# A mask moved from TensorE to VectorE, two heads' small operations joined, and a float8 product one unit later

## The chip, the cores and the metric

The kernel runs on one core of one Trainium2 chip. The metric is device time of one execution in microseconds (us). A core has five engines that work side by side, each through its own instructions in order: TensorE (PE, matrix products, with weight loads listed as PEld), VectorE (DVE), ScalarE (ACT), GpSimd (POOL) and SyncE (SP, which here only issues DMAs). They wait for each other through semaphores. Matrix products are written to PSUM, a small memory of eight banks; a bank holds 512 float32 per partition.

## The reference, cut to what matters

Input `x` is 4 batches of 1024 tokens with 512 features. The output is `x + attention(layernorm(x)) + float8_product(layernorm(x))`. Per batch, 16 heads of width 128:

```python
q  = rope(rmsnorm(xn @ Wq + bq));  lk = rope(rmsnorm(xn @ Wlk + blk));  lv = xn @ Wlv + blv
entries = softmax-weighted means of 4 tokens each            # 256 per batch
ck = rope(rmsnorm(entries @ Wk + bk));  cv = entries @ Wv + bv
sc = q @ ck.T * scale, where an entry that ends after the token gets -1e30
sparse = softmax over the 8 largest sc, times their cv
sl = q @ lk.T * scale over the token's own and the previous 128 tokens, masked to a band
local  = softmax(sl) @ lv
out = ((sparse + local) * 0.5) @ Wo + bo
```

The float8 branch rounds `xn * scale` and `input2 * scale1` to float8 values, and multiplies what was rounded.

## The kernel before, in words

A chunk is 128 tokens; there are 32 chunks `t`, 8 to a batch (`c` = 0 to 7). A unit is one pair of heads of one chunk: 8 units to a chunk (`u` = 0 to 7), 256 in all, numbered `n`. The tokens of a chunk sit in the 128 partitions. One main loop (L791) runs over steps `s`; the order of the instructions on every engine is exactly the order of the program. A step issues, for different units, a software pipeline:

- `scores(s, 0)` and `(s, 1)` (L563): TensorE writes, for each head, one 512-wide float32 PSUM tile `sc`: columns 0 to 127 scores with the previous chunk's keys (absent at `c` = 0), 128 to 255 with the own chunk's keys, and from 256 on the `m` = 32(c+1) compressed entries. A last small product, identity times mask (L583), adds -1e30 to the newest 32 entries that lie in the future. The tag `sc` has two buffers, one bank each.
- `keep_context(s-2)` (ACT), then `weigh(s, h)` for each head (L592): VectorE adds the band mask to the window's columns and finds the row's largest (L605), takes the eight largest entries (L608), negates the first (L610) and marks the eight taken ones in `taken` (`match_replace`, L611); ScalarE takes the exponentials of the window (L612) and of the entries (L620) from `sc` into `prob`.
- `queries(s+3)` (L440): TensorE's largest product, 8 instructions of 512 columns and a bias product.
- `settle(s, h)` (L623): VectorE zeroes the entries not taken and sums them (L627), guards and inverts the two sums (L636, L637), scales the entries (L638).
- `steps()`: one step of each running background generator: `chunk_prep` (layernorm, the entries of the chunk two ahead, 17 steps from `u` = 7) and `chunk_eight` (the float8 branch).
- `squares(s+3)` (ACT, L296) and `spread` (POOL: 1/sqrt by power, L290 and L291); `settle_window(s, h)` (ACT, L643, scales the window); `to_output(s-2)` (PE, L753); a second `steps()`.
- `turn(s)` (DVE, L661) transposes `prob` in 32x32 blocks and SP writes it to DRAM (L669); `values_of(s+1)` (PE, L537, into the shared two-buffer tag `pp`); `normalize(s+3)` (DVE L467, L310 to L312, with GpSimd's half of the rotation L309); `values(s-1)` (PE, L720, reads `probT` that came back from DRAM by `fetch`, L703); `turn_keys` and `fetch_keys` of `s+3`; `keep_values(s+1)` (ACT, L549).

The two background generators run in this way. `chunk_prep` of the chunk two ahead starts at `u` = 7 (layernorm statistics, L329, and 1/sqrt on GpSimd), normalizes at the next `u` = 0 (L337), turns at 1, multiplies at 2 (ScalarE copies the product `yp` to `y`, L361, then VectorE reads a column of it into `logits`, L363), ends at the next `u` = 7 with `cp`, copied by VectorE to `ckT` (L412, L414). `chunk_eight` of the own chunk starts at `u` = 5: three VectorE operations (L262 to L266) and GpSimd additions (L267, L269, L271, L273) at `u` = 5 and 6, the product `fp` (L425) in the first `steps()` of `u` = 7 and `f` (L430, L431) in the second. At `u` = 1 of the next chunk `to_output` adds the finished output to the residual (L762).

Of the kernel before, what the change touches and what calls it, by code (L numbers as in the profile page):

```python
# [12 lines left out]
F32 = mybir.dt.float32  # L13
BF16 = mybir.dt.bfloat16
U32 = mybir.dt.uint32
AF = mybir.ActivationFunctionType
ALU = mybir.AluOpType
AX = mybir.AxisListType

P = 128  # L20
# [10 lines left out]
TAKEN = 3e38  # L31
TAKEN_FROM = 1e38
# [6 lines left out]
def kernel(  # L39
# [26 lines left out]
    nc = tc.nc  # L66
# [5 lines left out]
    NE = P // RATIO  # L72
    NT = B * NCH
# [3 lines left out]
    const = ctx.enter_context(tc.tile_pool(name="const", bufs=1))  # L77
    work = ctx.enter_context(tc.tile_pool(name="work", bufs=2))
# [98 lines left out]
    picks = const.tile([P, NE], F32, name="picks")  # L177
    ident = const.tile([P, P], F32, name="ident")
    make_identity(nc, ident)
    ident_b = const.tile([P, P], BF16, name="ident_b")  # L180
    inv = const.tile([P, 1], F32, name="inv")
    bias_b = const.tile([P, 512], BF16, name="bias_b")
    nc.vector.memset(bias_b, 0.0)
# [250 lines left out]
    units = {}  # L434
# [115 lines left out]
        w["lv"] = lv  # L550


    heads = {}
    probs = [work.tile([P, 512], F32, name=f"prob_{h}", bufs=1) for h in range(2)]

    def columns(n):
# [6 lines left out]
    def scores(n, h):  # L563
        t, _ = place(n)
        c, m, loc, spa = columns(n)
        w = units[n]
        qT, lkT = w["qT"], w["lkT"]
        ckT, _ = entries[t // NCH]
        sc = psum.tile([P, 512], F32, tag="sc", name=f"sc_{n}_{h}")
        q = qT[:, :, h]  # L570
        if c:
            nc.tensor.matmul(
                blocks(sc[:, 0:P]),
                q,
                units[n - NU]["lkT"][:, :, ds(h * BLK, BLK)],
                start=True,
                stop=True,
            )
        nc.tensor.matmul(  # L579
            blocks(sc[:, P : 2 * P]), q, lkT[:, :, ds(h * BLK, BLK)], start=True, stop=True  # L580
        )
        nc.tensor.matmul(sc[:, spa], q, ckT[:, 0:m], start=True, stop=False)  # L582
        nc.tensor.matmul(  # L583
            sc[:, ds(2 * P + m - NE, NE)],
            ident_b,
            mask_b[:, 2 * P : 2 * P + NE],
            start=False,
            stop=True,
        )
        heads[n, h] = {"sc": sc}  # L590

    def weigh(n, h):  # L592
        c, m, loc, spa = columns(n)
        w = heads[n, h]
        sc = w.pop("sc")
        top = work.tile([P, 8], F32, tag="top", name=f"top_{n}_{h}")
        neg = work.tile([P, 2], F32, tag="neg", name=f"neg_{n}_{h}")
        tot = work.tile([P, 2], F32, tag="tot", name=f"tot_{n}_{h}", bufs=3)
        taken = work.tile([P, 2 * P], BF16, tag="taken", name=f"taken_{n}_{h}")
        prob = probs[h]  # L600
        if n % (NU * NCH) == 0:

            nc.gpsimd.memset(prob[:, 2 * P + NE : 4 * P], 0.0)

        nc.vector.tensor_tensor_reduce(  # L605
            sc[:, loc], sc[:, loc], mask_b[:, loc], -1.0, TAKEN, ALU.add, ALU.min, neg[:, 0:1]
        )
        nc.vector.max(top, sc[:, spa])  # L608

        nc.vector.tensor_scalar(neg[:, 1:2], top[:, 0:1], -1.0, 1e29, ALU.mult, ALU.min)  # L610
        nc.vector.match_replace(taken[:, 0:m], top, sc[:, spa], TAKEN)  # L611
        nc.scalar.activation(  # L612
            prob[:, loc],
            sc[:, loc],
            AF.Exp,
            bias=neg[:, 0:1],
            scale=-1.0,
            accum_out=tot[:, 0:1],
        )
        nc.scalar.activation(prob[:, spa], sc[:, spa], AF.Exp, bias=neg[:, 1:2])  # L620
        w.update(tot=tot, taken=taken, prob=prob)

    def settle(n, h):  # L623
        c, m, loc, spa = columns(n)
        w = heads[n, h]
        tot, taken, prob = w["tot"], w["taken"], w["prob"]
        nc.vector.scalar_tensor_tensor(  # L627
            prob[:, spa],
            taken[:, 0:m],
            TAKEN_FROM,  # L630
            prob[:, spa],
            ALU.is_ge,
            ALU.mult,
            accum_out=tot[:, 1:2],
        )
        nc.vector.tensor_scalar(tot, tot, 1e-9, None, ALU.max)  # L636
        nc.vector.reciprocal(tot, tot)  # L637
        nc.vector.tensor_scalar(prob[:, spa], prob[:, spa], tot[:, 1:2], None, ALU.mult)  # L638

    def settle_window(n, h):  # L640
        _, _, loc, _ = columns(n)
        prob, tot = heads[n, h]["prob"], heads[n, h]["tot"]
        nc.scalar.mul(prob[:, loc], prob[:, loc], tot[:, 0:1])  # L643

    def parts_of(n):

# [7 lines left out]
    def turn(n):  # L654
        parts = parts_of(n)
        g = len(parts)
        pb = work.tile([P, 1024], F32, tag="probB", name=f"probB_{n}", bufs=1)
        pb = of_heads(pb, n)
        for h in range(2):
            prob = heads.pop((n, h))["prob"]  # L660
            nc.vector.transpose(  # L661
                pb[:, :, ds(h * g, g), :],
                prob[:, parts[0] * P : (parts[-1] + 1) * P].rearrange(
                    "p (g b i) -> p b g i", b=NB, i=BLK
                ),
            )
        turned = dram.tile([P, 1024], F32, tag="pr", name=f"pr_{n}")
        turned = turned[:, 0 : NB * 2 * g * BLK]
        nc.sync.dma_start(turned, pb.rearrange("p b g i -> p (b g i)"))  # L669
        units[n]["pr"] = turned  # L670

    def turn_here(n):

        w, parts = units[n], parts_of(n)
        g = len(parts)
        w["tp"] = []
        for h in range(2):
            prob = heads.pop((n, h))["prob"]
            if h and g == 2:
                tp = tp[:, g * P :]  # L680
            else:
                tp = pp(f"tp_{n}_{h}")
            for i in range(g):
                nc.tensor.transpose(tp[:, ts(i, P)], prob[:, ts(parts[i], P)], ident)
            w["tp"].append(tp[:, 0 : g * P])
# [92 lines left out]
    def for_unit(n, *todo):  # L778
        if 0 <= n < NN:
            for f, *more in todo:  # L780
                f(n, *more)

    first, rounding = chunk_prep(0), round_w2()
    until(first, "A1")
    nc.vector.tensor_copy(ident_b, ident)
    until(first, "B2")
    small_constants()
    pick_tokens()
# [2 lines left out]
    for s in range(-3, NN + 2):  # L791
        t, u = place(s)

        if s == -2 or u == 7 and 0 <= t and t + 2 < NT:
            running = [*running[-2:], chunk_prep(t + 2)]
        if u == 3 and 0 <= t < NT:
            load_x(t, "sum")
        if u == 5 and 0 <= t < NT:
            running = [*running[-2:], chunk_eight(t)]
        if u == 4 and 0 <= t and t + 2 < NT:  # L800
            load_x(t + 2, "norm")

        for_unit(s, (scores, 0), (scores, 1))
        for_unit(s - 2, (keep_context,))
        for_unit(s, (weigh, 0), (weigh, 1))
        for_unit(s + 3, (queries,))
        if s + 2 < NU:
            for_unit(s + 2, (turn_keys_here,))
        for_unit(s, (settle, 0), (settle, 1))
        if s < 0:  # L810
            until(first, ("B3", "B4", "B6")[s + 3])
        steps()
        for_unit(s + 3, (squares, (0, 1, 2, 3)), (spread,))
        if s + 2 < NU:
            for_unit(s + 2, (keep_keys,))
        for_unit(s, (settle_window, 0), (settle_window, 1))
        for_unit(s - 2, (to_output,))
        steps()
        if by_dma(s):
            turn(s)  # L820
        if s == -1:
            until(first, "B7")
        for_unit(s + 1, (values_of,))
        if s == -1:
            until(first, "B8")
        if not by_dma(s):
            for_unit(s, (turn_here,))
        for_unit(s + 3, (normalize,))
        for_unit(s - 1, (values,))
        if by_dma(s):  # L830
            fetch(s)
        else:
            for_unit(s, (keep_turned,))
        if s + 3 >= NU:
            for_unit(s + 3, (turn_keys,), (fetch_keys,))
        for_unit(s + 1, (keep_values,))
        if s < NU:

            if s == -1:
                late_constants()  # L840
                for k in range(KK):
                    nc.scalar.dma_start(w2_raw[k], input2[ts(k, P), :])
            if 0 <= s < KK:
                for _ in range(4):
                    next(rounding, None)
            if 3 <= s + 6 < NU:
                load_wqk(s + 6, nc.scalar)
            if 3 <= s + 4 < NU:
                load_wlv(s + 4, nc.scalar)
            if 0 <= s + 1 < NU:  # L850
                load_wo(s + 1, nc.scalar)
        if u == 6 and 0 <= t and t + 2 < NT:
            load_angles(t + 2)
        units.pop(s - 1 - NU, None)
# [46 lines left out]
```

## Time and profile before

| | |
|---|---|
| time, median of 3 runs | 2831.97 us (2831.59 to 2832.27) |
| the profiled execution's own time | 2833.53 us |
| its span, first to last instruction | 2831.6 us |
| granted TensorE clock | 0.997 |
| busy: PE / DVE / ACT / POOL | 98% / 79% / 46% / 29% |
| DMA | 399.85 MB, 141 GB/s |

The span is the profiled execution from the first to the last instruction; the execution's own time is 1.9 us longer, and that time is 1.6 us above the median. A line of groups gives source line, engine, operation, tiles (out<-in), shape and count, then busy us and mean ns. A line of waits says who waited for whom: us in total, times, longest. A line of the timeline gives start, duration, engine and operation, and in brackets the idle time before it and what ended it. Busy shares are averages over the whole span.

### The profile page before, as it was taken

How to read it: one execution, taken by the hardware profiler on the slowest of the kernel's cores; microseconds unless marked ns; L12 is line 12 of the kernel's file. 1: busy time of each engine (PE TensorE's matmuls, PEld its weight loads, DVE VectorE, ACT ScalarE, POOL GpSimd, SP SyncE). 2: the span in 40 equal slices, each digit the busy share in tenths (PEclk: the TensorE clock that was granted, in tenths of full speed). 3: DMA queues.
4: the chain of work that ended last, by engine and by line, in shares of the span. 5: the costliest groups of instructions: out<-in, count | busy, mean ns of one | idle time of the engine just before them, and what ended most of it. 6: DMA issues, size and time to landing. Idle time of an engine off the chain costs nothing. (4 is left out here: it accounts for less than half of the span.)

```text
span 2831.6 us, 48506 instructions
## 1 busy us (share of the span) xinstructions
PE 2769.0 (98%) x12771; PEld 1873.8 (66%) x12969; DVE 2247.1 (79%) x9132; ACT 1299.1 (46%) x5075; POOL 821.3 (29%) x1161
## 2 busy tenths in 40 slices
PE   6999999999999999999999999999999999999998
PEld 4666666666666666666666666666666666667666
DVE  5777888888777778888877787888887777888886
ACT  3445444444444454444444444444444444444443
POOL 3432232322233322233223333223222233322221
PEclk9999999999999999999999999999999999999999
DMA  7345455555445445555544444555554544555553
GB/s 230 90 138 138 133 143 152 144 150 153 127 124 139 137 133 152 144 151 149 149 126 131 134 135 134 155 148 149 146 149 122 135 136 131 136 152 155 143 149 108
DMA packets 620850, 399.85 MB, mean 141 GB/s; under 512 B 306880, under 2 KB 573984, under 8 KB 620576
## 3 DMA queue, kind: packets, MB, share of 16 engines
q1 hardware_dynamic: 608352, 383.18, 48.8%
q10 hardware_dynamic: 12224, 13.56, 1.5%
q8 instruction: 105, 1.72, 0.3%
q14 instruction: 169, 1.38, 0.2%
HBM read 212.53 MB, written 184.03 MB: 140 GB/s over the span
## 5 line engine op out<-in xcount | busy, mean ns | idle before, releaser
L445 PE MATMUL qp<-wqk,xnT 128*128 128x512 f32 x2048 | 945.5, 604 | 4.9 <-DMA scales<-in_L_ffn_scale_dram 3.3
L445 PEld LDWEIGHTS qp<-wqk,xnT 128*128 128x128 f32 x2048 | 370.6, 191 | 385.2 <-issue 371.5
L612 ACT ACTIVATE prob<-sc,neg 128x256 f32<-128x256 f32 (+1 forms) x512 | 236.0, 461 | 779.6 <-DVE taken L611 759.3
L537 PEld LDWEIGHTS vp<-wlv,xnT 128*128 128x128 f32 x2048 | 386.5, 190 | 188.7 <-issue 94.0
L537 PE MATMUL vp<-wlv,xnT 128*128 128x256 f32 x2048 | 487.0, 381 | 17.2 <-DVE ckT L414 11.9
L753 PE MATMUL op<-wo,cT 128*128 128x512 f32 x1024 | 484.9, 596 | 7.1 <-ACT cT L735 1.5
L290 POOL TENSOR_SCALAR r<-ss 128x4 f32<-128x4 f32 x256 | 49.8, 194 | 1067.3 <-ACT junk L296 1059.3
L661 DVE STREAM_TRANSPOSE probB<-prob 128x512 f32<-128x512 f32 (+2 forms) x494 | 282.4, 609 | 92.5 <-ACT prob L643 89.1
L467 DVE SCALAR_TENSOR_TENSOR th<-qp,r,norm_w 128x128 f32<-128x128 f32 x1024 | 283.6, 339 | 71.0 <-POOL r L291 70.2
L309 POOL TENSOR_TENSOR rb<-th,cs 128x256 f32<-128x256 f32 x256 | 247.0, 965 | 278.0 <-DVE th L467 277.9
L296 ACT ACTIVATE junk<-qp 128x128 bf16<-128x128 f32 x1024 | 284.1, 277 | 88.0 <-remote 42.7
L549 ACT COPY lv<-vp 128x256 f32<-128x256 f32 x256 | 95.5, 373 | 477.6 <-PE cp L720 420.0
L753 PEld LDWEIGHTS op<-wo,cT 128*128 128x128 f32 x1024 | 188.9, 190 | 188.4 <-issue 113.9
L720 PE MATMUL cp<-probT,lv 128*128 128x128 f32 x1920 | 299.4, 276 | 4.4 <-DMA probT<-pr 4.4
L720 PEld LDWEIGHTS cp<-probT,lv 128*128 128x128 f32 x1920 | 276.1, 193 | 18.1 <-issue 5.2
L291 POOL TENSOR_TENSOR r<-r,nhalf 128x4 f32<-128x4 f32 x256 | 259.6, 1014 | 21.4
L720 PE MATMUL cp<-probT,cv 128*128 128x128 f32 x1536 | 256.7, 276 | 0.0
L582 PE MATMUL sc<-ckT,qT 128*128 128x96 f32 (+7 forms) x1024 | 226.5, 303 | 0.0
L643 ACT ACTIVATE prob<-prob,tot 128x256 f32<-128x256 f32 (+1 forms) x512 | 223.0, 484 | 3.6 <-DVE tot L637 3.6
L720 PEld LDWEIGHTS cp<-probT,cv 128*128 128x128 f32 x1536 | 214.3, 193 | 0.0
L605 DVE CUSTOM_DVE_ANT_0 sc<-sc,mask_b 128x256 f32<-128x256 f32 (+1 forms) x512 | 202.6, 396 | 7.2 <-PE sc L583 6.6
L579 PE MATMUL sc<-lkT,qT 128*128 128x128 f32 x1024 | 207.8, 285 | 0.0
(123 smaller groups left out, 3858.3 us busy)
## 6 DMA issues: line engine op xcount, KB each, us to landing
pr<-probB SPq DMA_DIRECT2D x127, 512.0 KB, 2.6
probT<-pr SPq DMA_DIRECT2D x508, 128.0 KB, 2.9
qk<-thb SPq DMA_DIRECT2D x992, 64.0 KB, 2.0
pr<-probB SPq DMA_DIRECT2D x96, 384.0 KB, 2.6
probT<-pr SPq DMA_DIRECT2D x384, 96.0 KB, 2.4
qT<-qk SPq DMA_DIRECT2D x248, 128.0 KB, 2.3
lkT<-qk SPq DMA_DIRECT2D x248, 128.0 KB, 2.5
x_norm<-_attn_hidden_states_dram SPq DMA_DIRECT2D x32, 256.0 KB, 3.2
```

The source lines that it names most:

```text
L291: nc.gpsimd.tensor_tensor(r, r, nhalf[: ss.shape[0], 0:n], ALU.pow)
L296: nc.scalar.activation(junk[: src.shape[0]], src, AF.Square, accum_out=acc)
L309: nc.gpsimd.tensor_tensor(bb, x12, wide(cs[:, HALF:ROPE]), ALU.mult)
L445: nc.tensor.matmul(qp, xnT[:, k, :], wqk_sb[u][:, k, :], start=(k == 0), stop=False)
L467: nc.vector.scalar_tensor_tensor(th[:, i, :], qp[:, ts(i, D)], r[:, i : i + 1], norm_w[:, i // 2, :], ALU.mult, ALU.mult,)
L537: nc.tensor.matmul(vp[:, 0:256], xnT[:, k, :], wlv_sb[u][:, k, :], start=(k == 0), stop=(k == KK - 1),)
L582: nc.tensor.matmul(sc[:, spa], q, ckT[:, 0:m], start=True, stop=False)
L612: nc.scalar.activation(prob[:, loc], sc[:, loc], AF.Exp, bias=neg[:, 0:1], scale=-1.0, accum_out=tot[:, 0:1],)
L643: nc.scalar.mul(prob[:, loc], prob[:, loc], tot[:, 0:1])
L661: nc.vector.transpose(pb[:, :, ds(h * g, g), :], prob[:, parts[0] * P : (parts[-1] + 1) * P].rearrange("p (g b i) -> p b g i", b=NB, i=BLK),)
L720: nc.tensor.matmul(blocks(cp[:, h, :]), v, probT[:, :, h * len(parts) + i - parts[0], :], start=(i == parts[0]), stop=(i == parts[-1]),)
L753: nc.tensor.matmul(op, cT[:, h, :], wo_sb[u][:, h, :], start=(u == 0 and h == 0), stop=(u == NU - 1 and h == 1),)
```

## The change

Five things are done:

1. The identity-times-mask product (L583) goes, with its bfloat16 identity. VectorE instead adds the mask to the newest 32 entries of both heads in one `tensor_tensor` in PSUM.
2. The heads' two `sc` tiles become one tile of two banks, with one buffer (`bufs=1`) in place of two.
3. `weigh` and `settle` handle both heads at once. The negation, the guard and the reciprocal become one instruction for both heads.
4. The order within `weigh` changes: band mask 0 and 1, the new addition, the eight largest 0 and 1, the negation; then on ScalarE both windows' exponentials and then both entries'; then `match_replace` of both heads, which now stands after the exponentials in the program. `settle_window` follows with both heads, as before.
5. `chunk_eight` starts at `u` = 6, so its product and its last step fall to `u` = 0 of the next chunk.

```diff
-        sc = psum.tile([P, 512], F32, tag="sc", name=f"sc_{n}_{h}")
+        if not h:
+            w["sc"] = psum.tile([P, 2, 512], F32, tag="sc", name=f"sc_{n}", bufs=1)
+        sc = w["sc"][:, h, :]
...
-        nc.tensor.matmul(sc[:, spa], q, ckT[:, 0:m], start=True, stop=False)
-        nc.tensor.matmul(
-            sc[:, ds(2 * P + m - NE, NE)],
-            ident_b,
-            mask_b[:, 2 * P : 2 * P + NE],
-            start=False,
-            stop=True,
-        )
+        nc.tensor.matmul(sc[:, spa], q, ckT[:, 0:m], start=True, stop=True)
...
+        for h in range(2):
+            nc.vector.tensor_tensor_reduce(
+                sc[:, h, loc], sc[:, h, loc], mask_b[:, loc],
+                -1.0, TAKEN, ALU.add, ALU.min, neg[:, h, 0:1],
+            )
+        last = sc[:, :, ds(2 * P + m - NE, NE)]
+        nc.vector.tensor_tensor(
+            last, last,
+            mask_b[:, 2 * P : 2 * P + NE].unsqueeze(1).to_broadcast([P, 2, NE]),
+            ALU.add,
+        )
+        for h in range(2):
+            nc.vector.max(top[:, h, :], sc[:, h, spa])
+        nc.vector.tensor_scalar(neg[:, :, 1], top[:, :, 0], -1.0, 1e29, ALU.mult, ALU.min)
+        for h in range(2):
+            nc.scalar.activation(probs[h][:, loc], sc[:, h, loc], AF.Exp,
+                bias=neg[:, h, 0:1], scale=-1.0, accum_out=tot[:, h, 0:1])
+        for h in range(2):
+            nc.scalar.activation(probs[h][:, spa], sc[:, h, spa], AF.Exp, bias=neg[:, h, 1:2])
+        for h in range(2):
+            nc.vector.match_replace(taken[:, h, 0:m], top[:, h, :], sc[:, h, spa], TAKEN)
...
+    def settle(n):
+        for h in range(2):
+            nc.vector.scalar_tensor_tensor(probs[h][:, spa], taken[:, h, 0:m], TAKEN_FROM,
+                probs[h][:, spa], ALU.is_ge, ALU.mult, accum_out=tot[:, h, 1:2])
         nc.vector.tensor_scalar(tot, tot, 1e-9, None, ALU.max)
         nc.vector.reciprocal(tot, tot)
+        for h in range(2):
+            nc.vector.tensor_scalar(probs[h][:, spa], probs[h][:, spa], tot[:, h, 1:2], None, ALU.mult)
...
-        if u == 5 and 0 <= t < NT:
+        if u == 6 and 0 <= t < NT:
             running = [*running[-2:], chunk_eight(t)]
```

## The prediction

> **What bounds the kernel now.** I read the page's busy times first, then the waits, then the timeline of one unit of the chunk `c` = 6 in the second batch (its VectorE cycles run from 1254.56 to 1346.09 us).
>
> ```profile
> PE 2769.0 (98%) x12771; PEld 1873.8 (66%) x12969; DVE 2247.1 (79%) x9132; ACT 1299.1 (46%) x5075; POOL 821.3 (29%) x1161
> ```
>
> TensorE is busy 98% of the span, so it sets the time now. VectorE's 79% looks like room. The waits say otherwise.
>
> ```profile
> ACT prob L612 <- DVE taken L611: 759.3, 488, 4.7
> DVE th L311 <- POOL rb L309: 159.1, 256, 0.6
> DVE probB L661 <- ACT prob L643: 89.1, 120, 1.5
> DVE th L467 <- POOL r L291: 70.2, 92, 3.2
> DVE logits L363 <- ACT y L361: 57.2, 31, 5.9
> DVE x_sum L762 <- PE op L753: 43.4, 32, 6.6
> DVE sc L605 <- PE sc L583: 6.6, 4, 6.1
> PE vp L537 <- DVE ckT L414: 11.9, 18, 1.1
> ```
>
> VectorE waits for its scores in only 4 units of 256: it trails TensorE nearly always, by 1 to 3 us. Of its 584 us idle (span less busy), 159 are a fixed wait for GpSimd's half of the rotation in every unit. Only the next four rows, 260 us, or 1.0 us per unit, can shrink. Each hangs on ScalarE, GpSimd or TensorE.
>
> The first row matters most. ScalarE's window exponential (L612) does not read `taken`, yet in 488 of 512 cases it starts when `match_replace` (L611) ends. Likewise L363 waits for ScalarE's L361 in 31 of 32 chunks, though it needs nothing that L361 writes. Both pairs read different columns of one PSUM bank. So two engines that touch one bank run one after the other in program order, in both directions.
>
> ```profile
> 1288.55 0.40 DVE L605 CUSTOM_DVE_ANT_0 sc<-sc,mask_b 128x256 f32<-128x256 f32 x1
> 1289.03 0.40 DVE L608 MAX8 top<-sc 128x8 f32<-128x224 f32 x1
> 1289.47 0.15 DVE L610 TENSOR_SCALAR neg<-top 128x1 f32<-128x1 f32 x1
> 1289.54 0.08 DVE L611 MATCH_VALUE_LOAD taken<-top,sc 128x8 f32 x1
> 1289.61 0.38 DVE L611 MATCH_REPLACE8 taken<-top,sc 128x224 bf16<-128x224 f32 x1
> 1289.90 0.42 DVE L605 CUSTOM_DVE_ANT_0 sc<-sc,mask_b 128x256 f32<-128x256 f32 x1
> 1290.10 0.47 ACT L612 ACTIVATE prob<-sc,neg 128x256 f32<-128x256 f32 x1 [2.12 <-DVE taken L611]
> ...
> 1290.57 0.44 ACT L620 ACTIVATE prob<-sc,neg 128x224 f32<-128x224 f32 x1
> ...
> 1291.29 0.38 DVE L627 SCALAR_TENSOR_TENSOR prob<-taken,prob 128x224 f32<-128x224 bf16 x1
> ...
> 1291.71 0.17 DVE L636 TENSOR_SCALAR tot<-tot 128x2 f32<-128x2 f32 x1
> ```
>
> A head's weighing costs VectorE 1.35 us (1288.55 to 1289.90), and both heads' settling starts 2.74 us after the unit's start and ends at 5.05.
>
> **TensorE's side.** The mask product takes one weight load per head: in the timeline of weight loads L583 starts at 2281.98 and the next matrix's load at 2282.10, 0.12 us; with rounding 0.11 x 512 = 56 us. At `u` = 7 three allocations of `pp` follow each other (`cp`, `fp`, `vp`), and `vp` waits for VectorE's copy of `cp`: 17 us idle before L537 in the groups. With `fp` in `u` = 0 that goes. TensorE's own line becomes 2832 - 73 = about 2760 us. The moved product itself (4 instructions, 0.9 us) is neutral.
>
> **VectorE's side, one unit of c = 6.** Durations are from the rows above, times from the unit's first L605. Band mask 0 at 0, band mask 1 at 0.47, the new addition at 0.95. The trace has no such addition. Bounds: 0.16 us (L414, 32 columns from PSUM) and 0.42 (L497, 256 columns); 64 columns lie near the first, so I take 0.22, with 0.03 to the next. Eight largest at 1.20, end 1.6. ScalarE's first window starts 0.12 later, as now (1289.99 to 1290.10): 1.7, the second window 0.47 later, 2.17, the first entries' exponential 2.64 to 3.08. `match_replace` of head 0 reads the same bank and stands behind it, so it cannot start before 3.1, while VectorE was free at about 2.1: a new stall of 1.0 us. Head 1 follows the last exponential at 3.43; settling starts at 3.8 instead of 2.74. Settling then saves a guard and a reciprocal, 0.2 us each start to start: two first operations 0.86, two joined 0.40, two last 0.62, so it ends at 5.7 instead of 5.05. The unit costs VectorE 0.67 us more although it runs two instructions fewer. With `c` = 0 (32 entries, window of 128: exponentials 0.37 and 0.28) the same steps give +0.55. The sign would change only if the stall were 0.67 shorter.
>
> Upper bound: if the two-bank tile were treated as a whole, both `match_replace` would stand behind all four exponentials, 0.4 to 0.8 us more. Lower: if the bank order did not hold, settling would still wait for the first entries' exponential (3.1), and the unit would cost 0.05 less than now at `c` = 6, 0.17 more at `c` = 0.
>
> The Trainium skill says the same of the bank (page "PSUM — Partial Sum Buffer", section "PSUM bank collisions raise a hardware error"): any two engines on one bank and 32 partitions must be kept apart, reads against reads included. That rule speaks against this change; by it the sum is the one below, without it the first rival's.
>
> **Waits that shrink or stay.** ScalarE ends its last exponential at 3.4 instead of 3.84. Waits behind ScalarE's later work therefore shrink by 0.67 + 0.4 at `c` = 6. At `u` = 0, 1, 3, 4 none is left. At `u` = 2 (L363) 1.5 becomes 0.5. At `u` = 5 squares follow the entries' copy and square (0.65): 0.4 stays. The float8 step brings 1.4 us of VectorE work and this chain: L266, GpSimd's addition 1.27, then its 1/sqrt 0.2 + 1.0, then L467; the waits with it (1.5 at `u` = 5 now) move to `u` = 6, as they hang on VectorE itself. At `u` = 7 VectorE loses L430 (0.74), but GpSimd's layernorm 1/sqrt and 1/sqrt still take as long: 0.4 becomes 1.1. So 3.5 us of waits stay per chunk.
>
> **Sum by chunk.** VectorE cycle of eight units (first L605 of a chunk to that of the next, second batch; mean of two batches), less its L661, L467, L363 and L762 waits in that window, plus eight units' extra, plus the waits that stay:
>
> | c | now | waits off | extra | stay | after | change |
> |---|---|---|---|---|---|---|
> | 0 | 78.8 | 11.2 | 4.4 | 5.8 | 77.8 | -1.0 |
> | 1 | 82.8 | 8.4 | 4.8 | 5.6 | 84.8 | +2.0 |
> | 2 | 84.6 | 8.6 | 4.9 | 5.3 | 86.2 | +1.6 |
> | 3 | 85.5 | 7.7 | 5.0 | 5.0 | 87.8 | +2.3 |
> | 4 | 88.2 | 6.7 | 5.2 | 4.2 | 90.9 | +2.7 |
> | 5 | 90.5 | 7.4 | 5.2 | 3.9 | 92.2 | +1.7 |
> | 6 | 91.5 | 6.5 | 5.4 | 3.5 | 93.9 | +2.4 |
> | 7 | 92.8 | 6.2 | 5.5 | 3.3 | 95.4 | +2.6 |
>
> Together +14.3, four batches +57, and +55 with the first and last chunk (no queries ahead in the last) at about nothing. In every chunk this line is above TensorE's (c = 6: 91.5 - 0.7 wait - 8 x 0.22 = 89.0). VectorE becomes the bound. Span 2831.6 + 55 = 2887; plus 1.9 for the execution, less 1.6 to the median: 2887 us.
>
> **Edits at nothing, and their cover.** One buffer of two banks: scores of the next unit must wait for the last reader of both heads. Now the reads end at 1292.39 and the next scores start at 1298.21; the last reader moves by 0.1. Gone only when VectorE trails by 7 us more. Turning, writing and fetching the probabilities: `probT` lands some 3 to 4 us before TensorE needs it; as VectorE falls behind that is used up and TensorE waits, which costs nothing more since TensorE is no longer the bound. SP's queue keeps its transfers and order; `chunk_eight` issues no DMA. `xn` at `u` = 0 takes the buffer of the float8 values, whose last GpSimd addition was queued before the rotation that VectorE waited for: nothing. `f` and its GpSimd addition (1.27) come a unit before L762 needs them: nothing.
>
> **Rivals.** *VectorE's stall isn't there* (the bank order doesn't hold for this order of readers, or is hidden): the extra falls by 0.4 to 0.8 per unit, of which a quarter comes back as waits behind ScalarE; the eight chunks sum to -15, four batches -60: some 2775 us, faster. It decides where the stall is under 0.3 us. For it: VectorE has fewer instructions. Against it: the two rows of waits. *TensorE stays the bound everywhere*, all of VectorE's extra in its 260 us of waits: 2760. For it: 0.67 x 256 = 172 is less than 260. Against it: the waits at `u` = 5 to 7 are made by VectorE's own work. *The tile is one for the order of readers*: 0.6 x 256 = 150 more, about 3020; for it speaks the single tile, against it that L612 runs beside L605 of the other head. *The mask product's time doesn't come back* (its load was hidden): TensorE's line stays at 2815, and nothing of the forecast changes.
>
> **How the numbers follow.** Forecast 0.74; no stall 0.14; TensorE bound 0.07; tile as one 0.05. The forecast's own range is 2840 to 2920: 0.05 us on each unit's extra is 13 us, 1 us on each chunk's waits 32. The whole range goes down to the first rival, 2775, and leaves out the 2760 and 3020 cases. A measurement here can tell 0.2% (5.7 us) from no change. Slower 0.75 (forecast without its lowest end, and tile as one), same 0.04, faster 0.21.
>
> **What would show it.** Right: VectorE's `match_replace` and with it L611's successor head the waits on ScalarE's entry exponential, about 1 us in all 256 units; TensorE shows 100 us or more idle before L720's successor, on `probT` DMAs; waits of L661 nearly vanish; the `u` = 6 unit takes 14 us. Wrong: `match_replace` directly behind the negation, TensorE still 97% busy. The likeliest error is in the waits at `u` = 5 to 7, which carry 3 us a chunk.

## The result and the profile after

The changed kernel takes 2972.24 us (median of four runs, 2971.69 to 2976.46) against 2832.09 us for the kernel before on the same chip. The ratio is 1.0498, interval 1.048 to 1.0517: 140 us, or 5.0%, slower. The forecast of 2887 us had the sign and the engine right; the time lies 52 us above the end of its range.

The busy times of the page, in the changed kernel:

```profile
PE 2809.7 (94%) x12457; PEld 1871.7 (63%) x12457; DVE 2148.0 (72%) x8619; ACT 1237.8 (42%) x5075; POOL 820.8 (28%) x1161
```

VectorE is busy for 99 us less than before (2148.0 instead of 2247.1) and runs 513 instructions fewer, and yet the span grew by 143 us, to 2974.7. TensorE lost its place as the bound: it is idle for 165 us (span less busy), 63 before. Busy shares alone would still name TensorE, at 94%. The waits of VectorE say which loop is closed:

```profile
DVE taken L631 <- ACT prob L629: 383.2, 256, 4.2
DVE th L310 <- POOL rb L308: 158.1, 256, 0.6
DVE th L466 <- POOL r L290: 102.8, 72, 3.1
DVE logits L362 <- ACT y L360: 28.8, 32, 7.0
DVE probB L677 <- ACT prob L659: 22.0, 30, 1.2
...
DVE x_sum L778 <- PE op L769: 6.8, 4, 5.2
...
DVE sc L598 <- PE sc L582: 4.1, 2, 2.9
```

The columns are total us, times, and longest. The first row is new: `match_replace` waits for the entries' exponentials in all 256 units, 1.5 us each. The last row says that VectorE waited for its scores in 2 units only, so TensorE is nearly always ahead of it. The four rows that the prediction called shrinkable (L467, L363, L661 and L762 before; L466, L362, L677 and L778 now) fell from 260 to 160 us together. The new row is nearly four times that fall.

The timeline of one unit (`c` = 6, `u` = 3, second batch), VectorE and ScalarE; columns are start, duration, engine, operation, and in brackets the idle time before and what ended it:

```profile
1353.58 0.40 DVE L598 CUSTOM_DVE_ANT_0 sc<-sc,mask_b 128x256 f32<-128x256 f32 x1
...
1353.90 0.13 DVE L598 DVE_READ_ACCUMULATOR2_ANT neg<- 128x1 f32 x1
...
1354.06 0.43 DVE L598 CUSTOM_DVE_ANT_0 sc<-sc,mask_b 128x256 f32<-128x256 f32 x1
...
1354.59 0.23 DVE L609 TENSOR_TENSOR sc<-sc,mask_b 128x64 f32<-128x64 f32 x1
1354.86 0.70 DVE L616 MAX8 top<-sc 128x8 f32<-128x224 f32 x2
...
1355.59 0.17 DVE L618 TENSOR_SCALAR neg<-top 128x2 f32<-128x2 f32 x1
1355.67 0.47 ACT L620 ACTIVATE prob<-sc,neg 128x256 f32<-128x256 f32 x1 [5.57 <-DVE top L616]
...
1356.13 0.46 ACT L620 ACTIVATE prob<-sc,neg 128x256 f32<-128x256 f32 x1
...
1356.58 0.78 ACT L629 ACTIVATE prob<-sc,neg 128x224 f32<-128x224 f32 x2
...
1357.40 0.09 DVE L631 MATCH_VALUE_LOAD taken<-top,sc 128x8 f32 x1 [1.64 <-ACT prob L629]
1357.48 0.38 DVE L631 MATCH_REPLACE8 taken<-top,sc 128x224 bf16<-128x224 f32 x1
...
1358.14 0.38 DVE L639 SCALAR_TENSOR_TENSOR prob<-taken,prob 128x224 f32<-128x224 bf16 x1
...
1359.29 0.58 DVE L651 TENSOR_SCALAR prob<-prob,tot 128x224 f32<-128x224 f32 x2
```

Read it as two hand-overs. ScalarE's first window (L620) needs only band mask 0, which was over at 1354.03, its minimum read out; it starts at 1355.67, after the eight largest of *both* heads (over at 1355.56). Head 0's `match_replace` (L631) needs nothing from ScalarE; it starts at 1357.40, after the entries' exponentials of *both* heads (over at 1357.36). The engines take turns on the pair of heads as a whole. Settling (L639) starts 4.56 us after the unit's first operation, where the kernel before had 2.74 and the prediction 3.8. Weighing and settling end 6.29 us after that operation (L651). In the kernel before they end at 5.05, counted from 1288.55 to the end of the second head's last operation:

```profile
1293.26 0.34 DVE L638 TENSOR_SCALAR prob<-prob,tot 128x224 f32<-128x224 f32 x1
```

TensorE's waits after, same columns:

```profile
PE cp L736 <- DMA probT<-pr: 58.5, 61, 3.6
PE sc L582 <- DVE ckT L413: 39.8, 30, 1.8
PE sc L572 <- DVE prob L639: 19.0, 17, 2.1
```

All three follow from VectorE's lateness, as far as the order of the program tells. The third is the single two-bank buffer: in 17 units the next scores wait behind a trailing VectorE and start 0.25 us past the end of its last `match_replace`.

By chunk, VectorE's cycle (first band mask of a chunk to that of the next, mean of the second and third batch) shows where the 140 us came from:

| c | 0 | 1 | 2 | 3 | 4 | 5 | 6 | 7 | sum |
|---|---|---|---|---|---|---|---|---|---|
| before | 78.8 | 82.8 | 84.6 | 85.5 | 88.2 | 90.5 | 91.5 | 92.8 | 694.7 |
| predicted | 77.8 | 84.8 | 86.2 | 87.8 | 90.9 | 92.2 | 93.9 | 95.4 | 709.0 |
| after | 80.9 | 85.7 | 87.9 | 89.6 | 93.5 | 95.8 | 97.7 | 99.7 | 730.7 |

730.7 less 694.7 is 36.0 per batch, times four 144: the loss is made in all chunks alike, the longer ones above all. Any bound would lengthen this cycle; that it is VectorE's own loop rests on the last row of its waits, 4.1 us for scores.

### The profile page after: what moved, and what is told of

Read it like the earlier page. It is cut to its first block, busy times and chain, and to the rows that moved or that the text cites. A ratio compares the mean times of both kernels' runs of the same rounds, so it can differ in the third digit from the quotient of the medians.

```text
span 2974.7 us, 46929 instructions
## 1 busy us (share of the span) xinstructions
PE 2809.7 (94%) x12457; PEld 1871.7 (63%) x12457; DVE 2148.0 (72%) x8619; ACT 1237.8 (42%) x5075; POOL 820.8 (28%) x1161
## 5 line engine op out<-in xcount | busy, mean ns | idle before, releaser
L620 ACT ACTIVATE prob<-sc,neg 128x256 f32<-128x256 f32 (+1 forms) x512 | 231.0, 456 | 1473.3 <-DVE top L616 1325.0
L444 PEld LDWEIGHTS qp<-wqk,xnT 128*128 128x128 f32 x2048 | 387.0, 196 | 388.9 <-issue 383.4
L736 PE MATMUL cp<-probT,lv 128*128 128x128 f32 x1920 | 308.5, 281 | 60.7 <-DMA probT<-pr 58.5
L466 DVE SCALAR_TENSOR_TENSOR th<-qp,r,norm_w 128x128 f32<-128x128 f32 x1024 | 281.1, 335 | 103.3 <-POOL r L290 102.8
L736 PEld LDWEIGHTS cp<-probT,lv 128*128 128x128 f32 x1920 | 270.1, 194 | 103.0 <-issue 86.5
L631 DVE MATCH_VALUE_LOAD taken<-top,sc 128x8 f32 x512 | 44.3, 87 | 383.2 <-ACT prob L629 383.2
L677 DVE STREAM_TRANSPOSE probB<-prob 128x512 f32<-128x512 f32 (+2 forms) x494 | 281.6, 607 | 22.0 <-ACT prob L659 22.0
L582 PE MATMUL sc<-ckT,qT 128*128 128x96 f32 (+7 forms) x1024 | 237.0, 314 | 39.8 <-DVE ckT L413 39.8
L736 PE MATMUL cp<-probT,cv 128*128 128x128 f32 x1536 | 259.7, 279 | 0.0
L736 PEld LDWEIGHTS cp<-probT,cv 128*128 128x128 f32 x1536 | 217.1, 196 | 0.0
L598 DVE CUSTOM_DVE_ANT_0 sc<-sc,mask_b 128x256 f32<-128x256 f32 (+1 forms) x512 | 205.0, 400 | 13.0 <-PE sc L582 4.1
```

The lines of the kernel that those rows point to most:

```text
L444: nc.tensor.matmul(qp, xnT[:, k, :], wqk_sb[u][:, k, :], start=(k == 0), stop=False)
L466: nc.vector.scalar_tensor_tensor(th[:, i, :], qp[:, ts(i, D)], r[:, i : i + 1], norm_w[:, i // 2, :], ALU.mult, ALU.mult,)
L620: nc.scalar.activation(probs[h][:, loc], sc[:, h, loc], AF.Exp, bias=neg[:, h, 0:1], scale=-1.0, accum_out=tot[:, h, 0:1],)
L677: nc.vector.transpose(pb[:, :, ds(h * g, g), :], prob[:, parts[0] * P : (parts[-1] + 1) * P].rearrange("p (g b i) -> p b g i", b=NB, i=BLK),)
L736: nc.tensor.matmul(blocks(cp[:, h, :]), v, probT[:, :, h * len(parts) + i - parts[0], :], start=(i == parts[0]), stop=(i == parts[-1]),)
```

## The experiments

The theory after the result: the two-bank tile counts as one in the order of engines, so that ScalarE and VectorE change over once per pair of heads. The rivals: the new VectorE addition, the joining of the small operations, the order within `weigh`, or the float8 step's new place. Each ratio is to the kernel before on the same chip.

### Two one-bank tiles in the changed kernel

```diff
-            w["sc"] = psum.tile([P, 2, 512], F32, tag="sc", name=f"sc_{n}", bufs=1)
-        sc = w["sc"][:, h, :]
+        sc = psum.tile([P, 512], F32, tag="sc", name=f"sc_{n}_{h}")
+        w.setdefault("sc", []).append(sc)
...
-        last = sc[:, :, ds(2 * P + m - NE, NE)]
-        nc.vector.tensor_tensor(
...
+        for h in range(2):
+            last = sc[h][:, ds(2 * P + m - NE, NE)]
+            nc.vector.tensor_tensor(last, last, mask_b[:, 2 * P : 2 * P + NE], ALU.add)
```

> The changed kernel, but each head has its own one-bank score tile again, and the newest entries' mask is added by two VectorE instructions, one per head; the order stays. Theory (the two-bank tile counts as one for the order of readers, so match_replace of head 0 stands behind all four exponentials and the first exponential behind both max): the wait of match_replace on ScalarE falls from 1.5 us to about 1.0 us per unit, it now starts when the first entries' exponential ends; one more small addition costs 0.2 us per unit; net 0.3 us x 256 = 75 us less, of which some comes back as waits behind ScalarE: 2905 to 2930 us. Rival (the order is kept per bank already, and the longer stall comes from ScalarE being late or from the small shared tiles neg and top): the wait stays at 1.5 us and the time is 2970 to 3020 us.

2798.94 us, ratio 0.9884 (0.9867 to 0.99): 173 us less than the changed kernel, and faster than the kernel before. The direction is the theory's; the gain is far more than it expected. The small tiles `neg` and `top`, which the rival suspected, are still shared here and do no harm. VectorE's wait for the entries' exponential in this kernel:

```profile
DVE taken L626 <- ACT prob L624: 254.5, 256, 1.3
```

That is 1.0 us per unit, the stall that the prediction had worked out for an order by bank. The timeline of the same unit in this kernel shows a second gain:

```profile
1275.03 0.40 DVE L597 CUSTOM_DVE_ANT_0 sc<-sc,mask_b 128x256 f32<-128x256 f32 x1
...
1275.35 0.46 DVE L597 CUSTOM_DVE_ANT_0 sc<-sc,mask_b 128x256 f32<-128x256 f32 x1
...
1275.72 0.38 DVE L609 TENSOR_TENSOR sc<-sc,mask_b 128x32 f32<-128x32 f32 x2
...
1276.51 0.47 ACT L615 ACTIVATE prob<-sc,neg 128x256 f32<-128x256 f32 x1 [4.55 <-DVE top L611]
...
1277.43 0.78 ACT L624 ACTIVATE prob<-sc,neg 128x224 f32<-128x224 f32 x2
...
1277.91 0.09 DVE L626 MATCH_VALUE_LOAD taken<-top,sc 128x8 f32 x1 [1.00 <-ACT prob L624]
...
1278.65 0.38 DVE L634 SCALAR_TENSOR_TENSOR prob<-taken,prob 128x224 f32<-128x224 bf16 x1
...
1279.80 0.58 DVE L646 TENSOR_SCALAR prob<-prob,tot 128x224 f32<-128x224 f32 x2
```

`match_replace` starts in the middle of the pair of exponentials (1277.43 to 1278.21), after head 0's alone. And VectorE's own operations overlap: band mask 1 starts 0.32 us after band mask 0 and before its end, where on the one tile it starts 0.48 after and behind it. The trace keeps for each instruction the semaphores that it waits for. On the one tile the second band mask waits, in all 256 units, for a semaphore that VectorE itself raises; on two tiles it waits only for TensorE's. So the order by tile stands in the program, as waits. Settling begins at 3.62 instead of 4.56, and the unit's weighing and settling take 5.35 us, not 6.29. Of the 173 us, 129 are the wait (383.2 less 254.5); the remaining 45 or so are, by subtraction, the lost overlap less what other waits gave back.

### One two-bank tile in the kernel before, nothing else

```diff
-        sc = psum.tile([P, 512], F32, tag="sc", name=f"sc_{n}_{h}")
+        if not h:
+            w["sc2"] = psum.tile([P, 2, 512], F32, tag="sc", name=f"sc_{n}", bufs=1)
+        sc = w["sc2"][:, h, :]
```

> The kernel before with one edit: the two heads' score tiles become one tile of two banks with one buffer. Nothing else moves. Theory (one tile, one order): VectorE's band mask of head 1 writes the other bank, yet stands behind both exponentials of head 0, which end 2.46 us after the unit's start at c = 6 (now it starts at 1.36): 0.8 to 1.1 us more per unit for VectorE, which becomes the bound: 2980 to 3040 us, and a wait of head 1's band mask on ScalarE's entry exponential in all 256 units. Rival (order per bank): no such wait, 2832 us within 0.5%.

3065.94 us, ratio 1.0826 (1.081 to 1.0842): 234 us from an edit that changes no computation, and above the theory's range. VectorE's and TensorE's waits in it:

```profile
DVE sc L607 <- ACT prob L622: 250.6, 256, 1.6
...
DVE sc L607 <- PE sc L585: 51.2, 32, 2.7
```

```profile
PE vp L537 <- DVE ckT L414: 151.7, 30, 5.9
```

Here head 1's band mask (L607) waits for a semaphore of ScalarE's and starts behind head 0's last exponential in every unit, though it works on the other bank. With it VectorE is late at `u` = 7, TensorE waits there for the copy of `cp` (151.7 us), and VectorE waits 51 us for late scores in turn.

### The mask product back on TensorE in the changed kernel

```diff
-        nc.tensor.matmul(sc[:, spa], q, ckT[:, 0:m], start=True, stop=True)
+        nc.tensor.matmul(sc[:, spa], q, ckT[:, 0:m], start=True, stop=False)
+        nc.tensor.matmul(
+            sc[:, ds(2 * P + m - NE, NE)],
+            ident_b,
+            mask_b[:, 2 * P : 2 * P + NE],
+            start=False,
+            stop=True,
+        )
...
-        last = sc[:, :, ds(2 * P + m - NE, NE)]
-        nc.vector.tensor_tensor(
...
```

> The changed kernel, with the newest entries' mask added by TensorE's product again and without VectorE's addition. Theory (VectorE bound): VectorE loses 0.26 us per unit, 66 us in all, TensorE gains 56 us which it has idle; some of it comes back as waits: 2905 to 2930 us. Rival (TensorE's line still counts, for example through its waits for probT): 2960 us or more.

2912.6 us, ratio 1.0285 (1.027 to 1.0301), as the theory expected. The joint addition on VectorE costs 60 us in the changed kernel, though it takes a product per head off TensorE. The wait of `match_replace` is nearly the same (383.2 us in the changed kernel), so the addition is a cost by itself and no cause of the stall:

```profile
DVE taken L632 <- ACT prob L630: 380.0, 256, 2.0
```

### The float8 step back at `u` = 5 in the changed kernel

```diff
-        if u == 6 and 0 <= t < NT:
+        if u == 5 and 0 <= t < NT:
```

> The changed kernel, float8 generator started at unit 5 again. Theory (VectorE's own line is the bound, and its wait for GpSimd's 1/sqrt behind the float8 additions goes with the generator wherever it starts): the 1.6 us wait moves back to unit 5 and takes that unit's 0.3 us wait with it, and the 0.74 us of the last float8 step again lie under unit 7's wait; 0.7 to 1.0 us x 32 chunks less: 2940 to 2955 us. Rival (the move pays, because it takes TensorE's wait for the buffer away): 2975 to 3000 us.

3006.95 us, ratio 1.0619 (1.0604 to 1.0635). The theory had a gain from this; it is a loss of 35 us, the rival's direction and 7 us above its range. VectorE's and TensorE's waits:

```profile
DVE sc L598 <- PE sc L582: 55.2, 38, 6.2
```

```profile
PE vp L536 <- DVE ckT L413: 146.4, 30, 6.6
```

With `cp`, `fp` and `vp` in a row on two buffers, TensorE stands at `vp` until a late VectorE has copied `cp`, and then VectorE stands for the next scores: a loop that TensorE's wait closes. That is read from the two rows.

### The float8 step at `u` = 6 in the kernel before

```diff
-        if u == 5 and 0 <= t < NT:
+        if u == 6 and 0 <= t < NT:
```

> The kernel before, with the float8 generator started at unit 6: the move alone. Theory (TensorE is the bound there, and the move takes away its 17 us before the values' product; VectorE loses the cover of the last float8 step, 0.74 us a chunk, but has some 2 us a chunk to spare): 2815 to 2830 us. Rival (the move only pays once VectorE trails, as in the changed kernel where undoing it cost 35 us): 2832 us within 0.2%, or above.

2814.33 us, ratio 0.9937 (0.9922 to 0.9952). This is just under the theory's range, and 18 us gained, where TensorE had stood 17 us idle at `vp`. VectorE pays for it: its wait for GpSimd's 1/sqrt (L467) grows from 70.2 to 104.5 us, but TensorE sets the time here, and the kernel is faster all the same.

### The mask on VectorE in the kernel before, head by head

```diff
-        nc.tensor.matmul(sc[:, spa], q, ckT[:, 0:m], start=True, stop=False)
-        nc.tensor.matmul(
-            sc[:, ds(2 * P + m - NE, NE)],
-            ident_b,
...
+        nc.tensor.matmul(sc[:, spa], q, ckT[:, 0:m], start=True, stop=True)
...
+        last = sc[:, ds(2 * P + m - NE, NE)]
+        nc.vector.tensor_tensor(last, last, mask_b[:, 2 * P : 2 * P + NE], ALU.add)
         nc.vector.max(top, sc[:, spa])
```

> The kernel before, with the newest entries' mask added by VectorE for each head in its own one-bank tile, and nothing else changed: the mask's move alone. TensorE loses 56 us. VectorE gains two additions, 0.2 us each at most, perhaps 0.1 where they overlap. Theory (VectorE is nearly as long as TensorE in the chunks from c = 4 on): half of the 56 us comes through: 2795 to 2825 us. Rival (VectorE has room): 2775 us.

2890.2 us, ratio 1.0205 (1.019 to 1.0221): slower, where faster was expected. TensorE now waits at `vp` for the copy of `cp` (11.9 us before), and in one head's chain each step stands behind the step before, though band mask and addition work on different columns of the tile:

```profile
PE vp L536 <- DVE ckT L413: 83.5, 30, 3.9
```

```profile
1314.57 0.40 DVE L597 CUSTOM_DVE_ANT_0 sc<-sc,mask_b 128x256 f32<-128x256 f32 x1
...
1315.05 0.20 DVE L601 TENSOR_TENSOR sc<-sc,mask_b 128x32 f32<-128x32 f32 x1
1315.29 0.40 DVE L602 MAX8 top<-sc 128x8 f32<-128x224 f32 x1
```

Band mask at 0, addition at 0.48, eight largest at 0.72, where the kernel before had the eight largest at 0.48. So a head costs VectorE 0.24 us more, a unit 0.47, and 256 units 120 us. That this takes VectorE's line past TensorE's is what the next run tests.

### The same with the float8 step at `u` = 6

> The kernel before with the mask added by VectorE per head and the float8 generator started at unit 6: the two moves together, without the joined operations and without the new order in weigh. Alone, the mask's move made it slower (2890 us) while TensorE waited 83 us before the values' product for VectorE's copy of cp, and the generator's move alone gained 18 us. Theory (that wait and the half clock after it were the whole loss): with it gone, 2795 to 2815 us. Rival (VectorE's two additions cost so much that it is the bound): 2835 us or more, with TensorE waiting for probT or for ckT instead.

2912.54 us, ratio 1.0285 (1.0269 to 1.03); the edit is the two diffs above together. The rival held: with the wait at `vp` gone the time does not fall, VectorE is the bound, and TensorE's waits only change their place:

```profile
PE sc L581 <- DVE ckT L413: 66.4, 30, 2.8
PE cp L714 <- DMA probT<-pr: 24.8, 33, 3.6
```

Here the later float8 step costs 22 us, after gains of 18 and 35 in two other kernels. The three agree with two terms. VectorE's line loses: its wait on GpSimd's 1/sqrt grows by 34 us in the kernel before, 25 here, 13 in the changed kernel. TensorE's line gains the wait at `vp`. Which one counts depends on who is late: TensorE sets the time in the kernel before; in the changed kernel TensorE's wait fed back to VectorE by 55 us; with the mask on VectorE it fed back by only 9 us (late scores, in the kernel one section up), so the loss stays. That reading is drawn from the waits, not from a run of its own.

### The settling joined in the kernel before

```diff
-    def settle(n, h):
+    def settle(n):
+        for h in range(2):
+            nc.vector.scalar_tensor_tensor(
+                probs[h][:, spa],
...
         nc.vector.tensor_scalar(tot, tot, 1e-9, None, ALU.max)
         nc.vector.reciprocal(tot, tot)
+        for h in range(2):
+            nc.vector.tensor_scalar(
+                probs[h][:, spa], probs[h][:, spa], tot[:, h, 1:2], None, ALU.mult
+            )
```

> The kernel before with settle for both heads at once (one guard and one reciprocal instead of two), each head's score tile and weighing as before: the joined small operations alone. Theory (TensorE is the bound, VectorE's 0.35 us per unit stay unused): 2832 us within 0.3%. Rival (VectorE's line counts through the waits behind it): 2815 us or less.

2852.48 us, ratio 1.007 (1.0053 to 1.0087): neither expectation; 512 VectorE instructions fewer and slower. VectorE's waits:

```profile
DVE prob L629 <- ACT prob L622: 188.0, 252, 1.0
```

In the kernel before, head 0's guard, reciprocal and scaling stood between the first operations of the two heads, and head 1's exponential ended while they ran. Joined, head 1's first operation (L629) comes up sooner and waits for its exponential, 0.75 us per unit. What was saved in instructions is lost in cover. Weighing and settling of a unit end 5.3 us after their start instead of 5.05.

### Exponentials and settling head by head, two tiles

```diff
         for h in range(2):
             nc.scalar.activation(
                 probs[h][:, loc],
...
-        for h in range(2):
             nc.scalar.activation(probs[h][:, spa], sc[h][:, spa], AF.Exp, bias=neg[:, h, 1:2])
         for h in range(2):
             nc.vector.match_replace(taken[:, h, 0:m], top[:, h, :], sc[h][:, spa], TAKEN)
...
-    def settle(n):
...
-        for h in range(2):
             nc.vector.scalar_tensor_tensor(
                 probs[h][:, spa],
...
```

Against the two-tile kernel; the lines taken out of `settle` stand at the end of `weigh`.

> The changed kernel with two one-bank tiles, ScalarE's exponentials by head (window and entries of head 0, then of head 1), and match_replace and the first settling operation by head. Theory: match_replace of head 0 can start 0.46 us earlier, as only two exponentials stand before it; that of head 1 starts when it does now, and one settling operation lies before it: 0.3 us less per unit for VectorE, of which TensorE's line lets half through: 2770 to 2790 us. Rival (TensorE is already the bound with two tiles): 2799 us within 0.3%.

2780.95 us, ratio 0.982 (0.9804 to 0.9837), as expected; the guard, reciprocal and last operations stay joined. It is 18 us under the same kernel with its exponentials by kind. The wait before `match_replace` falls from 254.5 to 141.7 us; it now stands behind two exponentials instead of three:

```profile
DVE taken L625 <- ACT prob L623: 141.7, 256, 1.2
```

### Entries first, two tiles

```diff
         for h in range(2):
+            last = sc[h][:, ds(2 * P + m - NE, NE)]
+            nc.vector.tensor_tensor(last, last, mask_b[:, 2 * P : 2 * P + NE], ALU.add)
+        for h in range(2):
+            nc.vector.max(top[:, h, :], sc[h][:, spa])
+        nc.vector.tensor_scalar(neg[:, :, 1], top[:, :, 0], -1.0, 1e29, ALU.mult, ALU.min)
+        for h in range(2):
+            nc.vector.match_replace(taken[:, h, 0:m], top[:, h, :], sc[h][:, spa], TAKEN)
+        for h in range(2):
+            nc.scalar.activation(probs[h][:, spa], sc[h][:, spa], AF.Exp, bias=neg[:, h, 1:2])
+        for h in range(2):
             nc.vector.tensor_tensor_reduce(
...
         for h in range(2):
-            last = sc[h][:, ds(2 * P + m - NE, NE)]
...
             nc.scalar.activation(
                 probs[h][:, loc],
...
-        for h in range(2):
-            nc.scalar.activation(probs[h][:, spa], sc[h][:, spa], AF.Exp, bias=neg[:, h, 1:2])
-        for h in range(2):
-            nc.vector.match_replace(taken[:, h, 0:m], top[:, h, :], sc[h][:, spa], TAKEN)
```

Against the two-tile kernel again: the same instructions in another order.

> The changed kernel with two one-bank tiles and another order in weigh: mask addition, eight largest, negation and match_replace of both heads first, then ScalarE's exponentials of the entries, then the band masks and the exponentials of the windows. Theory (match_replace stands behind the exponentials only because it comes later in the program): its wait goes; the band masks, now behind the entries' exponentials, wait 0.3 us at most; the unit costs VectorE 0.6 us less than with two tiles alone, and TensorE is the bound again: 2755 to 2780 us. Rival (settling waits for the window's sums instead, which come later now): 2790 to 2810 us, with the wait at the first settling instructions.

2770.48 us, ratio 0.9782 (0.9767 to 0.9796): the fastest kernel here, 62 us under the kernel before and 202 under the changed one. Its busy times and VectorE's waits:

```profile
PE 2723.1 (98%) x12291; PEld 1846.9 (67%) x12457; DVE 2102.1 (76%) x8875; ACT 1283.3 (46%) x5075; POOL 814.8 (29%) x1161
```

```profile
DVE tot L643 <- ACT prob L619: 68.7, 191, 0.5
DVE sc L608 <- ACT prob L606: 59.6, 256, 1.6
...
DVE sc L598 <- PE sc L581: 17.8, 33, 2.6
```

Everything VectorE does on the entries stands ahead of ScalarE's first read, so `match_replace` waits for nobody. The first band mask (L608) waits only for its own head's entries' exponential, 0.23 us a unit, and runs beside the other head's. VectorE waits for TensorE's scores again (33 units, at the addition, L598), and the time is that of TensorE's line, which the prediction had put at about 2760.

### The same with the float8 step at `u` = 5, and with one two-bank tile

The first edit is the one line shown above.

> The kernel with two tiles and the entries first (2770 us), float8 generator at unit 5 again. Theory (VectorE trails TensorE by 4 to 5 us there, so the values' product waits for its copy of cp, 2 us or more per chunk): 2800 to 2850 us. Rival (what the move gave in the kernel before, 18 us, is all): 2785 to 2795 us.

2787.38 us, ratio 0.9842 (0.9827 to 0.9856), the rival: where TensorE is the bound, the later float8 step is worth 17 us, its wait at `vp` (15.3 us here).

The second gives the entries-first kernel the two-bank tile and the joint addition of the changed kernel.

```diff
-        sc = psum.tile([P, 512], F32, tag="sc", name=f"sc_{n}_{h}")
+        if not h:
+            w["sc"] = psum.tile([P, 2, 512], F32, tag="sc", name=f"sc_{n}", bufs=1)
+        sc = w["sc"][:, h, :]
```

> The fastest version (entries first, 2770 us) with the one two-bank score tile and the joint mask addition of the changed kernel put back, order otherwise the same. Here match_replace stands before all exponentials, so the wait of the changed kernel cannot occur. Theory (the tile counts as one for every engine): the first band mask now stands behind both entries' exponentials, 1 us of wait where it was 0.2, and VectorE's operations on the two heads no longer overlap, 0.3 to 0.4 us: some 1 us more per unit on VectorE, which becomes the bound: 2870 to 2930 us. Rival (the two-bank tile only hurts where match_replace comes after the exponentials): 2770 to 2790 us.

3034.32 us, ratio 1.0714 (1.0696 to 1.0732): the theory's kind and far above its range, 264 us above the same order on two tiles where it had 100 to 160. VectorE's waits:

```profile
DVE sc L613 <- ACT prob L611: 200.5, 256, 1.4
DVE tot L648 <- ACT prob L624: 183.7, 256, 1.2
```

And the hand-over in the timeline of one unit:

```profile
1382.14 0.79 ACT L611 ACTIVATE prob<-sc,neg 128x224 f32<-128x224 f32 x2 [5.43 <-DVE taken L609]
...
1382.95 0.43 DVE L613 CUSTOM_DVE_ANT_0 sc<-sc,mask_b 128x256 f32<-128x256 f32 x1 [0.91 <-ACT prob L611]
```

The first band mask starts 0.02 us after both entries' exponentials are over. The two rows are 141 and 115 us longer than on two tiles; together 256, beside a loss of 264.

## Why the prediction was wrong in size

**Right.** VectorE's loop with ScalarE is the bound; the wait of `match_replace` is in all 256 units; L661's waits nearly vanish (89.1 to 22.0 us); TensorE falls idle by over 100 us. Smaller terms held too: the addition takes 0.23 us (0.22 taken); the waits that stay at `c` = 6 are 0.61, 0.31, 1.61 and 1.04 us at `u` = 2, 5, 6 and 7 (0.5, 0.4, 1.5, 1.1 predicted), so what the prediction called its likeliest error was none. The `u` = 6 unit takes 15.3 us there, where 14 was named. Taking the addition out gained 60 us; its step, 0.27 us in the unit shown (0.25 taken), times 256 is 69.

**The step that failed.** "`match_replace` of head 0 reads the same bank and stands behind it, so it cannot start before 3.1": the order was taken to go by bank. It goes by tile here. ScalarE's first window started at 2.09 us, after both heads' eight largest, where 1.7 was taken; `match_replace` started at 3.82, after both entries' exponentials, and settling at 4.56, not 3.8. The stall was 1.5 us per unit instead of 1.0. The rival *the tile is one for the order of readers* named the mechanism, with 0.05 for its chance. The argument against it, that L612 runs beside L605 of the other head, was drawn from a kernel in which the heads had separate tiles, so it said nothing on one tile. Where the trace of before could not show the case, the chance should have been nearer to even, and the range should have reached this rival's price.

**A second term, mis-sized the other way.** On two tiles, where the order by bank does hold, the forecast's 2887 should have come out, or a little more for the second addition; 2798.94 did. The stall was right (1.0 us per unit), but the unit's extra is 0.30 us at `c` = 6 (5.35 less 5.05), not 0.67: the VectorE operations were added one behind the other, and on separate tiles they overlap. 0.37 times 256 is 95 us. The chunk shows the same: at `c` = 6 the cycle on two tiles is 90.4 us where 93.9 was predicted, and eight times 0.37 is 3.0 of these 3.5. So the tile's 173 us and the 88 by which two tiles beat the forecast (2887 less 2799) met with opposite signs, and 173 less 88 is the miss of 85. The sign was right only because of the tile: the reasoning that the forecast was built on would have had it wrong.

**The rival's own price.** It said 150 us above the forecast, which makes 3037 and not the 3020 that stood beside it. The unit's end did come 0.59 us later than predicted in the unit shown (6.29 against 5.7), which is 151 over 256 units; the chunk table gives 22 per batch, 87 in all. The unit shown lies at `c` = 6. Taken as the mean of a chunk's units, the end comes 0.15 us later than predicted at `c` = 0 and 0.63 at `c` = 7, so the price of a long chunk was taken for all.

**The float8 step.** It was counted as 17 us for TensorE and 0.74 us per chunk against VectorE, so as a loss once VectorE is the bound. Both terms exist, but in the changed kernel it gains 35 us: without it TensorE waits 146.4 us at `vp`, and VectorE 55.2 us for scores.

**TensorE's waits.** That waiting "costs nothing more" held in the changed kernel, where VectorE waited 4.1 us for scores. It did not with the float8 step at `u` = 5 or with the two-bank tile in the kernel before, where 55 and 51 us came back. Their place was wrong as well: of 165 us idle, the `probT` DMAs account for 58.5; the copy of `cp` and the single buffer for another 59.

**The single buffer** was put at nothing, with 7 us to spare. The times given beside it leave 5.8 (1292.39 to 1298.21), and the first score product of that unit starts earlier still, at 1297.97. It was not nothing: TensorE's row for it is 19.0 us in 17 units.

**What stays open.** How much of the tile's cost the single buffer makes was not measured apart from the order of the readers. TensorE's waits that name it are small: 19.0 us here, 8.0 with the two-bank tile in the kernel before. Nor was it measured what the lower granted clock, described below, adds.

## What to carry to other kernels

Give heads that two engines work on in turn a tile each, even where one tile would save an instruction: one tile for both heads cost 173 to 264 us here through the waits that came with it. Put ahead of the other engine's reads whatever the trailing engine needs next, and before joining two heads' small operations look at which wait their alternation covers. When a trace has no case of what a change introduces, treat a rival that rests on it as open, however well the neighbouring rows fit.

## What the runs showed of the hardware

**VectorE's operations overlap where no wait of the program stands between them.** On two tiles the second band mask has no wait on the first: it starts 0.32 us after it (median of 256 units), while the first, of 0.40 us, still runs. On one tile, in different columns, it waits for VectorE's own semaphore and starts 0.49 us after the first (0.48 in the unit shown), once the first's accumulated value has been read.

**The granted clock falls when TensorE pauses.** The clock of the changed kernel against that of the one before:

```profile
core 0: 2974.7 us, clock 0.981
```

It was 0.997 before. In the trace's clock record this is made of 26 stretches at half speed, 114 us in all; the kernel before has 4, 21 us, at its start and end. The products bear it out: those of L736 follow each other at 0.11 us outside such stretches and at 0.21 within. All but the last, which lies past the program's end, begin within 5 us of the start of a pause of TensorE of 1.2 us or more: a pause of 2.04 us at 1501.9 was followed by 3.4 us at half speed from 1504.0. Pauses under 1.9 us that stood alone mostly had none, two of 1.42 and 1.24 us in a row (from 1029.9) had one, and the kernel with the mask on VectorE head by head had a pause of 3.21 us, from 654.2, without one. The Trainium skill's page "TensorE: Matmul & The Clock Gate" (section "Why this matters for your kernels") puts the idle time that drops the clock at some 3 us; in these runs 2 us could do it. Two of the slowest kernels spent more time so: 206 us with the two-bank tile in the kernel before, 189 us with the float8 step back at `u` = 5. That is a cost which a wait on TensorE can bring beyond its own length, but no run held the waits and changed the clock alone, so its part in the times was only argued.
